# Four graph layers on one core: where nodes' edges are counted, where sums of logits are fetched, and two tensors for a_dst

## The chip, the cores and the metric

The kernel runs on one core of one Trainium2 chip. The metric is the device time of one execution in microseconds. A core has five engines with a queue of instructions each: PE multiplies matrices, DVE and ACT work on vectors, POOL is used here for iotas, memsets and the gathers of indirect DMAs, and SP issues plain DMAs. Engines wait for one another by semaphores; each takes its own instructions strictly in order.

## What is computed

The graph has 6250 nodes and 106250 edges (50000 in both directions and a loop for each node), sorted by destination. A node's features x have 128 numbers. Cut to what matters:

```python
x = layernorm(x + mlp(concat(segment_sum(edge_attr_128, dst), x)))        # layer 0
h = (1 + eps) * x + segment_sum(x[src], dst)                              # layer 1
h = bn(relu(bn(h @ W1 + b1)) @ W2 + b2);  x = layernorm(x + relu(h + x))
h = relu(mean(x[src], dst) @ W1_l + b1 + x @ W1_r)                        # layer 2, two passes
x = layernorm(x + mean(h[src], dst) @ W2_l + b2 + h @ W2_r)
# layer 3: attention; every node has one more edge to itself, whose attribute is the
# mean of the attributes of its incoming edges
alpha = leaky_relu(a_src[row] + a_dst[col] + a_edge)                      # three heads
attn = softmax of alpha over the edges of one col
x = layernorm(x + (segment_sum(attn * xp[row], col) + gat_bias) @ lin_W + lin_b)
```

The kernel needs the following from the graph alone: for each node how many edges end at it (rcnt, its reciprocal), the number of its first edge (start_of) and of its last one (lasti). For layer 3 it needs the running sum of the edges' logits at each node's last edge (st), and a_dst of a node spread over all its edges.

## The kernel before

Nodes are held in 50 blocks of 125, and worked on in 13 chunks of four blocks. The edges lie 128 to a tile: 831 tiles. The program is recorded in the order in which the Python code runs and then placed by a scheduler of the framework, which estimates times and lets instructions of independent parts pass each other; the order on each engine is fixed when the program is built. Line numbers are those of the profile.

Most of the neighbour sums are a dense product. A matrix of edge counts (all 6250 sources by the first ND = 5000 destinations, `matrix`, bfloat16 in device memory) is built once and multiplied in layers 1 and 2; for the remaining 1250 destinations the rows of source nodes are gathered, 128 edges at a time.

- **Prologue (0 to about 95 us).** Indices are loaded and lists of keys made. Edst, the tensor in device memory to which a_dst will be written, is filled with zeros from `acc0` by ACT's queue.
- **Matrix build and layer 0's edge sums (95 to 485).** A loop over 70 batches `q`: each loads a piece of the 128-wide attributes (SP's queue), forms one-hots (`one_hots`, L352, DVE) and sums edges into `acc0` (PE L341, ACT L343, PE L345, DVE L348). From q=6 on, between the two halves of a batch, four steps of `making` run: two one-hots by DVE (olow and okey, L616), four matmuls (`made`, L643) and ACT's copy to `arena` (L645); a filled half of the arena is stored by ACT's queue. `products` (weights' products of layer 3) runs at q = 8 and 12.
- **Layer 0's MLP (485 to 637).** A loop over the 13 chunks: transposes (L308, copied by ACT L309), matmuls (L755, L756, ReLU by ACT L757; L763), layernorm, and `split` (L377 to L380) of the result into three bfloat16 parts in `xp`, a view of `arena`. Ahead of the loop stands POOL's memset of `xp[96:128]` (L740).
- **Layer 1's neighbours (637 to 1031).** `neighbours` multiplies `xp` with the matrix, streamed in pieces by SP's queue (L845), gathers the remaining rows (`row`, L800, POOL) and sums them as in the build. A hook `each(i)`, called once for every piece, drives two generators beside it: every seventh piece one step of `counting`, every third piece one step of `logits`. `counting` finds for 625 nodes a step how many edges lie before each (POOL's iota L542, seven compares by DVE L544 and L546, five matmuls of one column L536, then L430, L431, L539). `logits` loads the 16-wide attributes (`eat`, POOL's queue L691 and L693, with a memset L690 by POOL where a piece is not full) and multiplies and reduces them on DVE (L683, L684).
- **Layer 1's rest (1031 to 1163).** Two batch norms and matmuls, then a loop over the chunks with the layernorm and `split`. `counted` starts ahead of it with 50 gathers of destinations (`nd`, L436, POOL); in the loop each chunk adds three DVE instructions (L563 to L565), and at the end come start_of, rcnt and lasti. `loops` writes the running sums of logits to device memory as `esum`.
- **Layer 2's first pass (1163 to 1690).** `neighbours` again, with `last_sums` as its hook: one of 50 gathers of esum at lasti (`st`, L665, POOL) for a piece, any left over after it.
- **Layer 2's second pass (1690 to 2160).** `neighbours` with `then(k)` for each chunk: the layernorm, a_src and a_dst, POOL's memsets of the constant columns (xw L1048, ad L1049), and four indirect writes of a_dst to `edst` (L1071, POOL). A write to edst waits until the write before has landed.
- **Fill (2160 to 2223).** Edst is loaded in two DMAs and spread along the edges by scans (L1250, L1254); L1106 adds the edges' logits. Rows of layer 3 (L1090) are prefetched on POOL.
- **Layer 3 (2223 to 3562).** Attention over the tiles.

Of the kernel before, what the change touches and what calls it, by code (L numbers as in the profile page):

```python
# [8 lines left out]
F32 = mybir.dt.float32  # L9
# [200 lines left out]
def by_windows(ctx: ExitStack, tc: tile.TileContext, a: dict, out: bass.AP, consts, ix):  # L210
# [20 lines left out]
    mh = const.tile([128, H, F], F32, name="mh")  # L231
    cb = const.tile([128, F], F32, name="cb")
    x3 = dram.tile([NW, XW], F32, name="x3")
    edst = dram.tile([RB * L, 4], F32, name="edst")
    esum = dram.tile([RB * L, H], F32, name="esum")

    PARTS = [list(range(s, min(s + 2, N // SC))) for s in range(0, N // SC, 2)]
# [168 lines left out]
    mps = keep.enter_context(tc.tile_pool(name="mps", bufs=2, space=bass.MemoryType.PSUM))  # L406
    pp1 = keep.enter_context(tc.tile_pool(name="cps", bufs=1, space=bass.MemoryType.PSUM))
    nc.gpsimd.memset(acc0, 0.0)
    nc.scalar.dma_start(edst.rearrange("(p t) f -> p (t f)", t=L), acc0[:RB, 0:L * 4])
    loan = [NB5 * F // 2]  # L410

    def borrow(shape):
# [111 lines left out]
    def counting(pool, psum):  # L524


        row = tail[:RB, AN:AN + M * PB]
        view = arena[:RB, NB5 * 3 * F + 2 * (AN + M * PB):]
        steps = NB5 // M
        for c in range(steps + 1):  # L530
            if c:
                cs = slice((c - 1) * M, c * M)
                below = view[:, (c - 1) % 2 * M * PB:((c - 1) % 2 + 1) * M * PB]
                p = psum.tile([128, 2 * SC], F32, name="hp1")
                for i in range(M):
                    nc.tensor.matmul(p[:PB, i:i + 1], lhsT=below[:, i * PB:(i + 1) * PB], rhs=oneb,  # L536
                                     start=True, stop=True)
                start_row(n0[:PB, cs], p[:PB, 0:M])
                nc.vector.tensor_copy(n0i[:PB, cs], n0[:PB, cs])  # L539
            if c < steps:  # L540
                below = view[:, c % 2 * M * PB:(c % 2 + 1) * M * PB]
                nc.gpsimd.iota(row, pattern=[[1, M * PB]], base=c * M * PB + 1, channel_multiplier=0,  # L542
                               allow_small_or_imprecise_dtypes=True)
                nc.vector.tensor_scalar(below, row, ix["df"][:, 0:1], None, op0=OP.is_gt)  # L544
                for k in range(1, RT):
                    nc.vector.scalar_tensor_tensor(below, row, ix["df"][:, k:k + 1], below, op0=OP.is_gt, op1=OP.add)  # L546
            yield

    def counted(pool):


        thn = pool.tile([128, NB5], F32, name="node_col")
        nc.gpsimd.iota(thn, pattern=[[PB, NB5]], base=1, channel_multiplier=1,
                       allow_small_or_imprecise_dtypes=True)
        nc.vector.memset(upto[:, 0:1], 0.0)
        nd = pool.tile([128, NB5, 128], I32, name="nd")
        edges_from(a["dst"], n0i[:PB], nd[:PB])
        for blocks in CHUNKS:
            work = yield
            cs, nb = slice(blocks[0], blocks[-1] + 1), len(blocks)  # L560
            up = upto[:PB, 1 + cs.start:1 + cs.stop]
            lt = work.tile([128, 4, F], F32, name="rest")
            nc.vector.tensor_tensor(lt[:PB, :nb], nd[:PB, cs], over(thn[:PB, cs], 128), op=OP.is_lt)  # L563
            nc.vector.tensor_reduce(up, lt[:PB, :nb], AX.X, OP.add)
            nc.vector.tensor_add(up, up, n0[:PB, cs])  # L565

        shift = pool.tile([PB, 2, PB], F32, name="shifts")
        nxt = pool.tile([128, 2], F32, name="nexts")
        for i, by in enumerate((1.0, float(1 - PB))):
            nc.vector.tensor_scalar(nxt[:, i:i + 1], part, by, None, op0=OP.add)  # L570
            nc.vector.tensor_scalar(shift[:, i, :], iota[:PB, :PB], nxt[:PB, i:i + 1], None, op0=OP.is_equal)
        p = (yield).tile([128, 4, F], F32, name="node_p")[:, 0, :]
        start = p[:PB, 0:NB5]
        nc.tensor.matmul(start, lhsT=shift[:, 0, :], rhs=upto[:PB, 1:], start=True, stop=False)
        nc.tensor.matmul(start, lhsT=shift[:, 1, :], rhs=upto[:PB, 0:NB5], start=False, stop=True)
        nc.vector.tensor_copy(start_of[:PB], start)
        nc.vector.tensor_tensor(rcnt[:PB], upto[:PB, 1:], start, op=OP.subtract)
        nc.vector.reciprocal(rcnt[:PB], rcnt[:PB])
        nc.vector.tensor_scalar(lasti[:PB], upto[:PB, 1:], -1.0, None, op0=OP.add)
        yield  # L580
# [82 lines left out]
    def last_sums():  # L663
        for b in range(NB5):
            nc.gpsimd.indirect_dma_start(  # L665
                out=st[:PB, b, :], out_offset=None, in_=esum,
                in_offset=bass.IndirectOffsetOnAxis(ap=lasti[:PB, b:b + 1], axis=0))
            yield

    w1 = load_k(wp, "l0w1", a["L0_gnn_W1"], 2, 512)  # L670
    w2 = load_k(wp, "l0w2", a["L0_gnn_W2"], 4, F)
# [2 lines left out]
    def logits(pool, work):  # L674
# [11 lines left out]
        for c in range(0, L, W):  # L686
            x = work.tile([RB, W, 16], F32, name="eat")
            n = min(W, max(0, E - full - c))
            if n < W:
                nc.gpsimd.memset(x, 0.0)  # L690
            nc.gpsimd.dma_start(x[0:RB - 1], ea[0:full, :].rearrange("(p t) k -> p t k", t=L)[:, c:c + W, :])  # L691
            if n:
                nc.gpsimd.dma_start(x[RB - 1:RB, 0:n, :],  # L693
                                    ea[full + c:full + c + n, :].rearrange("(p t) k -> p t k", p=1))
            held.append((c, x))
            if len(held) > 2:
# [6 lines left out]
    ea = a["edge_attr_128"]  # L703
    of = bases(0, NG, DVE)
    make = making(mkp, mps)
    product = products()
    quads, batches, LATE = ND // SC * 13, (NG + 3) // 4, 6
    for q in range(batches):
        g0 = 4 * q
# [19 lines left out]
        next(sums, None)  # L729
        if q in (8, 12):  # L730
            next(product)
    for _ in make:
        pass
    keep.close()

    with tc.tile_pool(name="l0w", bufs=2) as work, \
            tc.tile_pool(name="hps", bufs=4, space=bass.MemoryType.PSUM) as hps, \
            tc.tile_pool(name="yps", bufs=2, space=bass.MemoryType.PSUM) as yps, \
            tc.tile_pool(name="tps", bufs=2, space=bass.MemoryType.PSUM) as tp:
        nc.gpsimd.memset(xp[96:128], 0.0)  # L740
        last = None
        for blocks in CHUNKS:
            b0, nb = blocks[0], len(blocks)
# [28 lines left out]

            def last(b0=b0, nb=nb, cs=cs):
                features(xt[:, cs], xn[:PB, b0:b0 + nb, :], tp)
        last()
    l0.close()

    def neighbours(before, take, then, table, after, each=None, bufs=5):
# [89 lines left out]
    with tc.tile_pool(name="l1", bufs=1) as wp:  # L868
# [37 lines left out]
        with tc.tile_pool(name="l1d", bufs=1) as dp, tc.tile_pool(name="l1e", bufs=4) as two, \  # L906
# [5 lines left out]
                for m in range(2):  # L912
                    stats(s1[:, m], k, hidden(k, m, hps))

            logit, indices = logits(dp, two), counting(dp, hps)

            def each(i):
                if i % 7 == 1:
                    next(indices, None)
                if i % 3 == 2:  # L920
                    next(logit, None)

            neighbours(None, take, then, tables[0], len(matrix), each)
            for x in (logit, indices):
                for _ in x:
                    pass
        counts = ExitStack()
        degrees = counted(counts.enter_context(tc.tile_pool(name="l1c", bufs=1)))
        next(degrees)
        with tc.tile_pool(name="l1p", bufs=1) as lp, tc.tile_pool(name="l1w", bufs=2) as work, \  # L930
                tc.tile_pool(name="hps", bufs=3, space=bass.MemoryType.PSUM) as hps:
            looped = loops(lp, hps)
# [2 lines left out]
            for k in range(len(PARTS)):  # L935
# [10 lines left out]
                stats(s2, k, hp[:, :w])  # L946
                if k in (2, 4):
                    next(looped)
        batchnorm(2, s2, b2, g2, be2)
        with tc.tile_pool(name="l1x", bufs=2) as work, tc.tile_pool(name="zps", bufs=3, space=bass.MemoryType.PSUM) as zps, \  # L950
                tc.tile_pool(name="tps", bufs=2, space=bass.MemoryType.PSUM) as tp:
            last = None
            for blocks in CHUNKS:
# [6 lines left out]
                z = nodes(h0[:, cs], nb, zps)  # L960
                if last is not None:
                    last()
                degrees.send(work)
                layernorm(xn[:PB, b0:b0 + nb, :], z)
                keep_nodes(nc.sync, tables[1], blocks, xn[:, b0:b0 + nb, :])
                split(xn[:PB, b0:b0 + nb, :], blocks, work)
# [1 line left out]
                def last(b0=b0, nb=nb, cs=cs):  # L968
                    features(xt[:, cs], xn[:PB, b0:b0 + nb, :], tp)
            last()  # L970
            degrees.send(zps)
        counts.close()

    with tc.tile_pool(name="l2", bufs=1) as wp, tc.tile_pool(name="l2w", bufs=2) as work, \
# [47 lines left out]
                keep_nodes(nc.scalar, tables[2], blocks, pn[:, b0:b0 + len(blocks), :])  # L1024
            return late

        ends = last_sums()
        neighbours(before, take, None, tables[1], len(matrix), lambda i: next(ends, None))
        for _ in ends:
            pass  # L1030


    with tc.tile_pool(name="l2bw", bufs=2) as work, \
            tc.tile_pool(name="tps", bufs=2, space=bass.MemoryType.PSUM) as tp, \
            tc.tile_pool(name="aps", bufs=1, space=bass.MemoryType.PSUM) as aps:
        for blocks in CHUNKS:
            split(pn[:PB, blocks[0]:blocks[-1] + 1, :], blocks, work)

# [3 lines left out]
        def then(k):  # L1042
            blocks = CHUNKS[k]
            b0, nb = blocks[0], len(blocks)
            x = xn[:PB, b0:b0 + nb, :]
            xw = work.tile([128, 4, XW], F32, name="xw")
            ad = work.tile([128, 4, 4], F32, name="ad")
            nc.gpsimd.memset(xw[:, :, F + H:XW], 1.0)  # L1048
            nc.gpsimd.memset(ad, 0.0)  # L1049
            s = nodes(xt[:, cols(k)], nb, tp)  # L1050
            y = work.tile([128, 4, F], F32, name="y3")
            y = y[:PB, :nb, :]
# [16 lines left out]
            lrelu(lg)  # L1069
            for j in range(nb):  # L1070
                nc.gpsimd.indirect_dma_start(  # L1071
                    out=edst, out_offset=bass.IndirectOffsetOnAxis(ap=start_of[:PB, b0 + j:b0 + j + 1], axis=0),
                    in_=ad[:PB, j, :], in_offset=None)
            keep_nodes(nc.scalar, x3, blocks, xw)

# [21 lines left out]
        fetch(b)  # L1097
    with tc.tile_pool(name="fill", bufs=1) as fp, \
            tc.tile_pool(name="fps", bufs=2, space=bass.MemoryType.PSUM) as pp:
        ed = fp.tile([RB, L, 4], F32, name="ed")  # L1100
        for p0, p1, queue in ((0, 112, nc.sync), (112, RB, nc.scalar)):
            queue.dma_start(ed[p0:p1].rearrange("p t f -> p (t f)"),
                            edst[p0 * L:p1 * L, :].rearrange("(p t) f -> p (t f)", t=L))
        filled = fp.tile([RB, L, H], F32, name="filled")
        along(tc, consts, ix["first"], [ed[:, :, h] for h in range(H)], [filled[:, :, h] for h in range(H)], fp, pp)()
        nc.vector.tensor_add(filled, filled, aeb)  # L1106
# [812 lines left out]
```

## Time and profile before

| what | value |
|---|---|
| median of 5 runs | 3557.95 us (3534.11 to 3571.18) |
| profiled execution | 3564.12 us |
| its span | 3562.3 us |
| mean granted TensorE clock | 0.847 |
| busy: PE, DVE, ACT, POOL | 2697.9, 1736.0, 904.2, 1685.0 us |
| DMA | 461.80 MB, 130 GB/s mean |

The span runs from the first to the last recorded instruction; the profiled execution is one run, and its time lies some us beside its span. Busy times overlap, as the engines work side by side. A row of a group of instructions gives the line, engine, operation, output and inputs, shape and count, then the busy time in us and the mean of one in ns, then how long the engine idled before these instructions and what ended it. A row of waits gives the waiting engine, tile and line, what it waited for, and the us in total, the number of times and the longest. "issue" is idle time in which the engine waited for nothing that the profile shows. The granted clock is given as a share of full speed.

### The profile page before, as it was taken

The page shows a single profiled execution, that of the slowest core. Times are in us where ns is not written, and L with a number is a line of the kernel's source. Part 1 is how long each engine was busy: PE and PEld are TensorE (multiplying, and loading weights), DVE is VectorE, ACT ScalarE, POOL GpSimd, SP SyncE. Part 2 cuts the span into 40 slices and gives each one's busy share as a digit, 9 for nine tenths or more (in the row PEclk, how much of TensorE's full clock was granted, in tenths as well). Part 3 has the DMA queues.
Part 4 walks back from the last instruction along what each step waited for, and adds up shares of the span by engine and source line. Part 5 has one row for each costly group of instructions (what it writes and reads, how often), then busy time and mean ns, then how long its engine had stood idle before and what let it go on. Part 6 is the DMA issues. An engine that isn't in the chain of part 4 may idle for free.

```text
span 3562.3 us, 42918 instructions
## 1 busy us (share of the span) xinstructions
PE 2697.9 (76%) x14960; PEld 1648.5 (46%) x14960; DVE 1736.0 (49%) x4633; ACT 904.2 (25%) x1661; POOL 1685.0 (47%) x1690
## 2 busy tenths in 40 slices
PE   2889989799994589999888894666666666666666
PEld 1444456344442135444334342555555555555555
DVE  4877854584138100001211123666666666656666
ACT  0788854000014000002000010222222222222222
POOL 5000020576433764520666425666666666666563
PEclk9888889899995589999888896888777777777777
DMA  5799931676632355553555552222222222222221
GB/s 168 233 302 294 301 133 45 200 237 210 214 102 61 109 160 188 183 176 108 181 167 172 158 173 76 54 57 58 58 56 61 58 57 57 56 56 60 53 58 35
DMA packets 334828, 461.80 MB, mean 130 GB/s; under 512 B 45310, under 2 KB 219166, under 8 KB 334245
## 3 DMA queue, kind: packets, MB, share of 16 engines
q1 hardware_dynamic: 251420, 278.88, 26.1%
q0 software_dynamic: 54912, 105.86, 11.0%
q10 hardware_dynamic: 28270, 74.24, 5.6%
q8 instruction: 119, 1.95, 0.2%
q14 instruction: 107, 0.88, 0.1%
HBM read 375.30 MB, written 83.36 MB: 129 GB/s over the span
## 4 chain that ended last, share of the span: by engine, by line
PE 39%; issue 11%; DVE 10%; another core or an unknown queue 4%; POOL 3%; ACT 1%; DMA 1%; DVEq 0%; ACTq 0%; POOLq 0%; SPq 0%
PE sums L845 17%; PE o L1198 8%; PE w_p L1176 3%; POOL rows L1090 2%; PE o L1148 2%; DVE w L1186 2%; PE yp L1020 1%; PE both L341 1%; DVE mx L1179 1%; PE both L1183 1%; ACT w L1188 1%; DVE w L1171 1%; PE fp L1132 1%; DVE acc L1206 1%
## 5 line engine op out<-in xcount | busy, mean ns | idle before, releaser
L845 PE MATMUL sums<-piece,arena 125*128 125x500 bf16 x4500 | 1036.3, 386 | 62.0 <-issue 50.5
L1090 POOL DMA_INDIRECT rows<-x,srca x831 | 852.8, 1026 | 481.9 <-issue 213.3
L845 PEld LDWEIGHTS <-arena 125*128 125x128 bf16 x4500 | 438.2, 99 | 613.5 <-issue 153.4
L800 POOL DMA_INDIRECT row<-table,srca x549 | 541.4, 986 | 332.1 <-PE both L341 143.9
L1198 PE MATMUL o<-rows,w 128*120 128x132 f32 x2078 | 406.4, 340 | 160.9 <-ACT w L1188 83.4
L1198 PEld LDWEIGHTS o<-rows,w 128*120 128x120 f32 x2078 | 355.4, 239 | 201.5 <-ACT w L1188 104.3
L645 ACT CAST arena<-made 128x1000 bf16<-128x1000 f32 (+1 forms) x260 | 315.9, 1280 | 61.1 <-PE made L643 57.8
L1188 ACT ACTIVATE w<-w 128x720 f32<-128x720 f32 x208 | 167.0, 803 | 639.0 <-DVE w L1186 498.3
L643 PE MATMUL made<-okey,olow 128*128 128x250 bf16 x1000 | 257.6, 400 | 35.5 <-ACT arena L645 17.4
L1179 DVE TENSOR_REDUCE mx<-w_p 120x1 f32<-120x768 f32 x208 | 198.3, 953 | 172.3 <-PE o L1198 70.3
L1176 PE MATMUL w_p<-ident,w 128*120 128x128 f32 x1248 | 231.3, 328 | 22.4 <-issue 16.6
L1183 PE MATMUL both<-ident,mx 120*128 120x120 f32 x208 | 74.1, 356 | 214.6 <-DVE acc L1206 110.5
L1186 DVE TENSOR_TENSOR w<-w,both 128x720 f32<-128x720 f32 x208 | 187.2, 900 | 89.6 <-PE w_p L1176 56.2
L343 ACT COPY by_node<-both 128x128 f32<-128x128 f32 (+1 forms) x48 | 12.8, 266 | 813.2 <-PE both L341 589.4
L1176 PEld LDWEIGHTS w_p<-ident,w 128*120 128x120 f32 x1248 | 189.9, 170 | 62.8 <-issue 30.8
L352 DVE TENSOR_TENSOR onehot<-iota,relg 128x384 f32<-128x384 f32 x118 | 63.9, 544 | 304.3 <-PE both L341 219.1
L1171 DVE TENSOR_TENSOR w<-oh,z 128x720 f32<-128x720 f32 x208 | 187.3, 900 | 14.7 <-PE o L1198 8.0
L643 PEld LDWEIGHTS <-olow 128*128 128x128 bf16 x1000 | 109.9, 119 | 157.3 <-issue 69.1
L716 POOL MEMSET ea<- 128x128 f32 x1 | 0.2, 206 | 362.8 <-DMA ea<-in_edge_attr_dram 362.8
L616 DVE TENSOR_TENSOR okey<-iok,key 128x1000 bf16<-128x1000 bf16 (+1 forms) x260 | 169.8, 653 | 0.0
L1148 PE MATMUL o<-zeros 128*120 128x380 bf16 x416 | 145.2, 400 | 22.5 <-issue 21.9
L348 DVE TENSOR_TENSOR arena<-arena,both 128x32 f32 x183 | 34.2, 187 | 236.2 <-PE both L345 137.2
(286 smaller groups left out, 3387.7 us busy)
## 6 DMA issues: line engine op xcount, KB each, us to landing
piece<-edges SPq DMA_DIRECT2D x300, 625.0 KB
edges<-arena ACTq DMA_DIRECT2D x100, 625.0 KB
ea<-in_edge_attr_dram SPq DMA_DIRECT2D x69, 768.0 KB
loop<-x SPq DMA_DIRECT2D x208, 68.0 KB
rows<-x,srca POOLq DMA_INDIRECT x831
row<-table,srca POOLq DMA_INDIRECT x549
eat<-in_edge_attr_dram POOLq DMA_DIRECT2D x28, 236.0 KB
table<-xn SPq DMA_DIRECT2D x24, 224.0 KB
```

What stands on the lines that cost most here:

```text
L643: nc.tensor.matmul(p[:, i, 0:NB5 * GD], lhsT=o[:, :, i], rhs=w[:, :, i], start=True, stop=True)
L645: nc.scalar.copy(to, p[:, 0:n, 0:NB5 * GD].rearrange("p i (h d) -> p i h d", d=GD))
L800: nc.gpsimd.indirect_dma_start(out=r[:, j, :], out_offset=None, in_=table, in_offset=bass.IndirectOffsetOnAxis(ap=ix["src"][:, t:t + 1], a ...
L845: nc.tensor.matmul(p, lhsT=xp[:PB, h, i, :], rhs=t[:PB, :, (h - h0) * SC:(h - h0 + 1) * SC], start=(h == 0 and i == 0), stop=(h == NB5 - 1 ...
L1090: nc.gpsimd.indirect_dma_start(out=r[:, j, :], out_offset=None, in_=x3, in_offset=bass.IndirectOffsetOnAxis(ap=ix["src"][:, BT * b + j:BT ...
L1148: nc.tensor.matmul(to, lhsT=zeros[:, 0:H * BW], rhs=zeros[:, 0:to.shape[1]], start=True, stop=True)
L1171: nc.vector.tensor_tensor(w, oh.to_broadcast([128, S, H, BW]), z.rearrange("p j (h w) -> p j h w", w=1).to_broadcast([128, S, H, BW]), op= ...
L1176: nc.tensor.transpose(tp[:, j // 3, j % 3 * 128:(j % 3 + 1) * 128], w[:, j, :, :].rearrange("p h w -> p (h w)"), ident)
L1179: nc.vector.tensor_reduce(mx, tp[:, :, 0:384], AX.XY, OP.max)
L1186: nc.vector.tensor_tensor(wf, wf, mb.rearrange("p (j h) w -> p j (h w)", j=1) .to_broadcast([128, S, H * BW]), op=OP.subtract)
L1188: nc.scalar.activation(wf, wf, AF.Exp)
L1198: nc.tensor.matmul(o[:, 0:F + H + 1], lhsT=wf[:, j, :], rhs=rr, start=(j == 0), stop=(j == S - 1))
```

## The change

Five things change. `counting` moves from layer 1's neighbours to the build loop: one step each at q = 15, 20 and so on to 65, with row and view tiles of its own. `counted` moves from layer 1's rest to layer 0's MLP: its gathers ahead of the loop, its DVE work in the loop's chunks, its tail behind it. `last_sums` moves from layer 2's first pass to the middle of layer 1's rest, ahead of the second batch norm. The attributes `eat` are loaded by ACT's queue, and their memset is DVE's. a_dst is written to two tensors in turn, both filled with zeros at the start and added up in the fill; and the constant columns of xw and ad are set once, in tiles with room for three chunks, by DVE.

```diff
-    edst = dram.tile([RB * L, 4], F32, name="edst")
+    edst = [dram.tile([RB * L, 4], F32, name=f"edst{i}") for i in range(2)]
...
-    nc.scalar.dma_start(edst.rearrange("(p t) f -> p (t f)", t=L), acc0[:RB, 0:L * 4])
+    for x in edst:
+        nc.scalar.dma_start(x.rearrange("(p t) f -> p (t f)", t=L), acc0[:RB, 0:L * 4])
...
     def counting(pool, psum):
-        row = tail[:RB, AN:AN + M * PB]
-        view = arena[:RB, NB5 * 3 * F + 2 * (AN + M * PB):]
+        row = pool.tile([RB, M * PB], F32, name="node_row")
+        view = pool.tile([RB, 2 * M * PB], BF16, name="node_below")
...
-                p = psum.tile([128, 2 * SC], F32, name="hp1")
+                p = psum.tile([128, 256], F32, name="counts")
...
     def last_sums():
         for b in range(NB5):
             nc.gpsimd.indirect_dma_start(out=st[:PB, b, :], ..., in_=esum, ...)
-            yield
...
             if n < W:
-                nc.gpsimd.memset(x, 0.0)
-            nc.gpsimd.dma_start(x[0:RB - 1], ...)
+                nc.vector.memset(x, 0.0)
+            nc.scalar.dma_start(x[0:RB - 1], ...)
             if n:
-                nc.gpsimd.dma_start(x[RB - 1:RB, 0:n, :], ...)
+                nc.scalar.dma_start(x[RB - 1:RB, 0:n, :], ...)
...
-    product = products()
+    product, indices = products(), counting(gw, pp1)
     for q in range(batches):
...
+        if q >= 13 and q % 5 == 0:
+            next(indices, None)
-    for _ in make:
-        pass
+    for x in (make, indices):
+        for _ in x:
+            pass
     keep.close()
...
         nc.gpsimd.memset(xp[96:128], 0.0)
+        degrees = counted(cp)
+        next(degrees)
         for blocks in CHUNKS:
...
+            degrees.send(work)
         last()
+        degrees.send(yps)
     l0.close()
...
-            logit, indices = logits(dp, two), counting(dp, hps)
+            logit = logits(dp, two)
             def each(i):
-                if i % 7 == 1:
-                    next(indices, None)
...
-        degrees = counted(counts.enter_context(tc.tile_pool(name="l1c", bufs=1)))
-        next(degrees)
...
                 if k in (2, 4):
                     next(looped)
+            last_sums()
         batchnorm(2, s2, b2, g2, be2)
...
                     last()
-                degrees.send(work)
                 layernorm(xn[:PB, b0:b0 + nb, :], z)
...
-        ends = last_sums()
-        neighbours(before, take, None, tables[1], len(matrix), lambda i: next(ends, None))
-        for _ in ends:
-            pass
+        neighbours(before, take, None, tables[1], len(matrix))
...
+        ads = xws.tile([128, 3, 4, 4], F32, name="ad")
+        xws = xws.tile([128, 3, 4, XW], F32, name="xw")
+        nc.vector.memset(xws[:, :, :, F + H:XW], 1.0)
+        nc.vector.memset(ads, 0.0)
...
-            xw = work.tile([128, 4, XW], F32, name="xw")
-            ad = work.tile([128, 4, 4], F32, name="ad")
-            nc.gpsimd.memset(xw[:, :, F + H:XW], 1.0)
-            nc.gpsimd.memset(ad, 0.0)
+            xw, ad = xws[:, k % 3], ads[:, k % 3]
...
-                    out=edst, out_offset=...
+                    out=edst[j % 2], out_offset=...
...
-        ed = fp.tile([RB, L, 4], F32, name="ed")
-        for p0, p1, queue in ((0, 112, nc.sync), (112, RB, nc.scalar)):
-            queue.dma_start(ed[p0:p1], edst[p0 * L:p1 * L, :])
+        ed, more = (fp.tile([RB, L, 4], F32, name=n) for n in ("ed", "edm"))
+        for to, x, queue in ((ed, edst[0], nc.sync), (more, edst[1], nc.scalar)):
+            for p0, p1 in ((0, 112), (112, RB)):
+                queue.dma_start(to[p0:p1], x[p0 * L:p1 * L, :])
+        nc.vector.tensor_add(ed, ed, more)
```

The order that the scheduler makes of it, on POOL: the nd gathers stand around the memset of `xp[96:128]`, 17 before it and 33 behind it. The 50 st gathers stand between the rows of layer 1 and those of layer 2, which then come in one run. In the build, DVE's compares of `counting` alternate one by one with the one-hots of `making`.

## Prediction

> **What bounds the kernel now.** I read the windows by stage first (us from the span's start; busy time of each engine, granted clock, DMA share and rate; the matrix build, layer 0's MLP, the end of layer 1, then layer 2's two passes):
>
> ```profile
> 300.00:400.00 100.00, 90.11 (x677) 45.14 (x676) 80.36 (x222) 82.82 (x86) 0.00 (x0) 0.86 0.92 301
> 485.00:560.00 75.00, 70.12 (x334) 45.93 (x333) 37.02 (x101) 30.74 (x52) 19.43 (x5) 0.95 0.19 60
> 1085.00:1163.00 78.00, 31.60 (x104) 21.03 (x104) 76.96 (x257) 32.77 (x65) 21.76 (x17) 0.51 0.21 54
> 1200.00:1300.00 100.00, 66.36 (x225) 23.96 (x225) 4.09 (x13) 3.21 (x7) 75.88 (x68) 0.65 0.37 100
> 1300.00:1500.00 200.00, 196.49 (x1070) 96.78 (x1068) 17.80 (x55) 12.41 (x28) 100.74 (x104) 0.99 0.61 194
> 1760.00:2045.00 285.00, 241.71 (x1272) 110.84 (x1270) 44.55 (x190) 15.21 (x37) 160.47 (x170) 0.87 0.54 166
> ```
>
> PE sets the pace nearly everywhere. Three stages are worse than PE needs: the end of layer 1 (1085 to 1163) is DVE's, at 77 of 78 us; 1200 to 1300 has PE at 66% and a clock of 0.65, where the same loop 100 us later runs at 98% and 0.99; and 1760 to 2045 is alike in mild form. In both, POOL is the busy one. The build is PE's, with DVE and ACT close behind.
>
> Next the groups by line (busy, mean ns | idle before) of the moved work:
>
> ```profile
> L546 DVE SCALAR_TENSOR_TENSOR arena<-arena,df 119x625 bf16<-119x625 f32 x45 | 39.0, 866 | 0.4
> L563 DVE TENSOR_TENSOR rest<-nd,node_col 125x512 f32<-125x512 int32 (+1 forms) x13 | 8.6, 665 | 0.1
> L564 DVE TENSOR_REDUCE upto<-rest 125x4 f32<-125x512 f32 (+1 forms) x13 | 8.6, 661 | 0.0
> L436 POOL DMA_INDIRECT nd<-in_dst_dram,n0i x50 | 63.3, 1265 | 15.1 <-issue 14.5 <-DVE xn L956 0.3 <-DVE rstd L298 0.3
> L665 POOL DMA_INDIRECT st<-esum,lasti x50 | 59.9, 1199 | 66.7 <-DVE lasti L579 51.7 <-issue 15.0
> L1071 POOL DMA_INDIRECT edst<-ad,start_of x50 | 59.8, 1196 | 157.3 <-DMA edst<-ad,start_of 76.2 <-issue 46.3 <-DVE xw L1067 19.2
> ```
>
> A gather costs POOL 1.2 us and 0.3 us of issue, 1.5 in all: the 50 nd gathers are 75 us, the 50 st gathers again. Then the chains of waits, of the build (first two lines), of 1163 to 1300 (third), of 1690 to 2160 (the rest):
>
> ```profile
> DVE olow L616 <- PE made L643: 44.5, 100, 1.1
> PE made L643 <- DVE olow L616: 13.1, 23, 0.9
> ...
> PE sums L845 <- issue: 29.7, 31, 2.2
> ...
> POOL edst L1071 <- DMA edst<-ad,start_of: 76.2, 32, 4.4
> DVE xw L1066 <- POOL xw L1048: 53.6, 10, 9.5
> PE both L341 <- issue: 29.5, 38, 2.4
> PE ad_p L1061 <- ACT x3t L309: 13.8, 2, 7.0
> ```
>
> Last, the timeline of POOL where layer 0's MLP begins (start, us):
>
> ```profile
> 488.62 16.09 POOL L740 MEMSET arena<- 32x19200 bf16 x1 [43.55 <-ACT xc L309]
> 504.78 1.38 POOL L792 MEMSET arena<- 128x1532 f32 x1
> 506.11 0.67 POOL L542 IOTA arena<- 119x625 f32 x1
> ```
>
> **The sum, against the profiled execution:** 3564.1 us, a span of 3562.3 and 1.8 around it. That is 6.2 above the median of 3557.95, so the total below is lowered by 6. A measurement of this kernel can tell about 0.5%, 18 us.
>
> **Start.** Zeroing edst is doubled, 1.7 MB more by ACT's queue beside the first loads; at the 253 GB/s of 100 to 200 that is 7 us at most. I take +2 (0 to 6).
>
> **Build.** Ten counting steps come in, one every fifth batch from q=15. One is 0.55 us (L544), six L546 of 0.87 and some 0.55 us of small ones: 6.3 us of DVE, 63 in all. DVE idles 82 us between 100 and 485 (by windows of 100, 100, 100 and 85 us), but a batch takes 6.0 us, of which DVE is free 1.3. So one step fills the free time of five batches and DVE stands at 97%. It hides only if DVE works ahead: it does, its 44.5 us of idle before L616 is waiting for PE to give a buffer back, and three make buffers at 1.46 us each let it lead by 4.4 us of the 6.3. But the changed program alternates L546 with the one-hots, PE's 13.1 us of waiting for them grows, and the sums' chain through L348 lies behind the same queue. Bounds: 0, if all hides, and +63, if none does. I take +20, nearer to the low end, because DVE's lead covers two thirds of a step; for the range 5 to 45.
>
> **Layer 0's MLP.** Thirteen us of counting leave DVE, 13 x 1.5 us of degrees come in; DVE is busy 37 of 75, so both cost nothing (up to 19 if not covered). What costs is POOL's order: the 16.1 us memset of arena, which the first split (ACT L377) needs, now stands behind 17 nd gathers. 484 + 17 x 1.5 = 509.5, and 16.1 more: 525.6. Before, the split ran at 508.69, and only because DVE had waited 8.56 us for the iota behind the memset; now it could run at 502.5 and waits to 525.6. Behind it on ACT are the evictions of the next chunk's features and hidden units, so PE, after some 8 us of work that needs none, stands about 15 us, where it stood 4.9: +12 (0 to 20). The other 33 gathers take 50 us beside 110 us of PE work: hidden.
>
> **Layer 1's neighbours.** DVE loses 48 us of counting, the eat loads leave POOL for ACT, which is idle there. PE is busy 364 of 394 us, and of its 30 only the DVE waits (6.8 at 702) and part of the crawl at 660 to 673 can go: −8 (−20 to +6; the loss if ACT, waiting for an eat buffer, holds by_node's copy, L343). [...]
>
> **Layer 1's rest.** From the DVE-bound 78 us go L563 to L565, 8.6 + 8.6 + 1.9, and a tail of some 2 us: −20. Late next is PE at 32 and ACT at 33, so nothing takes it back (−26 to −8). The st gathers come here: esum's write is issued at 1062.9, so they run from 1065 to 1140, and the rows are due at about 1150. If POOL's 1265 ns of nd beside this DVE work (986 ns for a row) holds for them, they end at 1144, still in time. [...]
>
> **Layer 2's first pass.** Five st gathers go from before the first row: −7. The slow stretch 1196 to 1241 and 1260 to 1287 coincides with POOL issuing 45 st and the rows without pause; PE then starts one instruction per 0.7 us. Of 137 us from 1163 PE idles 51. The start of layer 1's pass, rows alone, idles 19 of 63 at a clock of 0.85 and 10 of the next 120. So about 25 of the 51 go, and of PE's 86 us at 0.66 about 15 more: −40 with the −7 counted in (−60 to −5). The low end is the case in which rows alone crowd PE as much.
>
> **Layer 2's second pass.** POOL waits 76 us for the write before to land, and while it does it can't issue rows or the memset of xw, for which DVE waits 53.6, and PE through ACT 13.8. Two tensors halve the first (each waits for the one before last), three standing tiles end the second. PE idles 67 of 470 us; 13.8 + half of the 29.5 of L341 + a little clock: −30 (−60 to 0).
>
> **Fill.** Edst's last write moves ahead of the rows of layer 3 that stood between: before 2184.7, now some 6 us earlier. Two loads of 1.7 MB instead of one (9.2 us at 185 GB/s; two at the 301 of the build 11.3): +2; one add of 119x3584, from L1106's 3.0 us for 119x2688: +4. Sum 0 (−6 to +8). Layer 3 is as it was.
>
> 2 + 20 + 12 − 8 − 20 − 40 − 30 + 0 = −64; 3564 − 64 − 6 = 3494.
>
> **Rivals.**
> A. As forecast, 3494 (3440 to 3538): 0.62.
> B. PE's crawl comes of POOL's row bursts themselves, and the gathers were hidden: for it, layer 1's pass crawls at 660 to 673 with no st gather. Layer 2 gives the −7 and −13.8 alone: 2 + 20 + 12 − 8 − 20 − 21 = −15, so 3543 (3535 to 3560): 0.18.
> C. Slower: DVE becomes the build's bound. Its place is 170 to 480, its price up to 6.3 us a step, +63, and the path's L348 behind it. With the start's 2 and layer 0's 12 that is 77 against 28 from layer 1; it decides from where layer 2 gives under 49 us. With 30 there: +19, 3577 (3555 to 3590): 0.20. For it: DVE at 81% with 16% more to do. Against it: the 44.5 us in which DVE waits for PE.
>
> The range for 8 in 10 takes all of A but its lowest end, B, and C to 3570: 3445 to 3570; A's own range stands above. Faster by over 0.5% (under 3540): nearly all of A, a third of B and none of C: 0.66. Within: the rest of A, half of B, a tenth of C: 0.13. Slower: 0.21.
>
> **What would show it.** Right: the build ends 15 to 30 us later with PE's wait for DVE olow grown from 13.1; POOL's 16 us memset starts near 510 and PE has a gap of 15 us behind it; no st gather among layer 2's rows, and PE over 80% in the 137 us from its start; the edst wait under 40. Wrong: a build longer by 45 or more, rows still crawling after the first 25, or a first row later than 10 us after layer 1's end.

## The result: a little slower, and the profile after

The changed kernel takes 3582.91 us in the median of 35 runs, the kernel before 3565.04 in 61: a ratio of 1.0052, 95% interval 1.004 to 1.0065. The forecast was 3494, with a range of 3445 to 3570. The profiled execution has a span of 3585.2 us against 3562.3. The kernel before took 3242 to 3248 us beside e1 to e4, e9 to e12, e17 and e18 (group S, where PE's products have next to no idle time put down to issue: in e4 at most 0.8 us before `sums` and 0.1 before layer 3's `o`) and 3551 to 3565 beside the others and in the traces here (group L, where the kernel before has 50.5 and 77.1), so stages are compared only within a group, and kernels by their ratio to the kernel before.

The stages of the two profiled executions, marked off by PE's instructions (first and last product of the build, last of layer 0, first and last of each pass over the matrix), in us:

| stage | before | after | measured | forecast |
|---|---|---|---|---|
| start to the first make | 96.9 | 102.9 | +6.0 | +2 |
| build | 382.3 | 407.3 | +25.0 | +20 |
| layer 0's MLP | 151.8 | 161.8 | +10.0 | +12 |
| from there to layer 1's pass | 10.5 | 21.3 | +10.8 | none |
| layer 1's pass (neighbours) | 389.8 | 454.3 | **+64.5** | **−8** |
| layer 1's rest and layer 2's first pass | 625.6 | 542.9 | −82.7 | −60 |
| to the second pass | 33.2 | 34.7 | +1.5 | 0 |
| layer 2's second pass | 470.4 | 456.5 | −13.9 | −30 |
| fill, to layer 3's first z | 53.0 | 56.8 | +3.8 | 0 |
| layer 3 | 1348.8 | 1346.7 | −2.1 | 0 |

One stage has turned the gain into a loss: without its +64.5 the stages add up to −42. The windows of the changed kernel (columns as in the prediction; the build, then the middle of layer 1's pass), and last the middle of that pass in the kernel before:

```profile
300.00:400.00 100.00, 83.51 (x649) 44.25 (x648) 87.16 (x233) 77.71 (x78) 1.97 (x3) 0.74 0.83 276
820.00:920.00 100.00, 64.47 (x299) 28.14 (x296) 53.60 (x80) 0.80 (x3) 34.99 (x36) 0.82 0.56 174
...
820.00:920.00 100.00, 98.75 (x566) 46.19 (x564) 29.97 (x72) 1.33 (x5) 62.52 (x62) 1.00 0.67 213
```

In 820 to 920 of the changed kernel no engine is busy for more than 65 of 100 us; there is a wait, not a load. Over the whole pass PE idles 77 us where it idled 26. The waits from 680 to 1105 name the cause:

```profile
DVE product L683 <- DMA eat<-in_edge_attr_dram: 86.0, 21, 8.6
...
PE both L341 <- DVE arena L348: 32.5, 3, 11.7
...
PE both L345 <- ACT by_node L343: 11.8, 2, 9.4
```

DVE stands 21 times, in all 86 us, before an attribute load; behind it in DVE's queue is the addition of a row's sum (L348), and PE waits for that. The other side is ACT's issues of these loads (L691 loads 118 partitions, L693 the last one; count, then the time that an issue holds ACT, min/median/max in ns), and ACT's timeline:

```profile
L691 ACTq DMA_DIRECT2D eat<-in_edge_attr_dram x28: 239/258/7906, 681.9 to 894.7; - x28
L693 ACTq DMA_DIRECT2D eat<-in_edge_attr_dram x17: 393/4547/9402, 682.2 to 816.4; - x17
```

```profile
705.15 5.96 ACTq L693 DMA_DIRECT2D eat<-in_edge_attr_dram  x1
...
736.04 7.33 ACTq L693 DMA_DIRECT2D eat<-in_edge_attr_dram  x1
743.72 0.27 ACT L343 COPY by_node<-both 128x128 f32<-128x128 f32 x1 [62.70 <-DMA row<-table,srca]
```

Issuing a load took POOL 0.53 to 0.57 us. On ACT most issues of the 118 partitions take 0.26 us (the longest 7.9), but the issue of the one partition that follows holds ACT for 4.5 us in the median; the 45 issues together hold it for 120 us. The copy of by_node, which PE needs, stands behind them: at 743.72 it follows a 7.33 us issue at once. What the queue itself does is in the DMA part of 697 to 700 (packets, MB, share of the 16 engines), with the queue of POOL's loads in the kernel before, 671 to 675, in the last line:

```profile
q0 software_dynamic: 64, 0.13, 13.2%
q10 hardware_dynamic: 67, 0.13, 11.6%
...
q0 software_dynamic: 370, 0.81, 68.3%
```

ACT's queue (q10) moved nothing but these loads and had 11.6% of 16 engines: not quite two. From POOL (q0) the same loads had 68.3%. Theory W, in the next section, puts this down to the count of partitions. The kernel before has a load of 112 partitions in its fill, the one of edst by SP's queue: from 2188 to 2192 that queue (q1), with nothing else to move, had 89.7%. The experiments test it.

### The profile page after: what moved, and what is told of

It reads as the page before. It is cut to its first block, busy times and chain, and to the rows that moved or that the text cites. A ratio compares the mean times of both kernels' runs of the same rounds, so it can differ in the third digit from the quotient of the medians.

```text
span 3585.2 us, 42898 instructions
## 1 busy us (share of the span) xinstructions
PE 2684.4 (75%) x14960; PEld 1648.5 (46%) x14960; DVE 1753.6 (49%) x4648; ACT 909.8 (25%) x1661; POOL 1650.1 (46%) x1607
## 4 chain that ended last, share of the span: by engine, by line
PE 56%; DVE 15%; issue 10%; DMA 7%; another core or an unknown queue 6%; ACT 4%; ACTq 1%; DVEq 1%; POOL 0%; SPq 0%; POOLq 0%
PE sums L852 22%; PE o L1197 9%; DMA eat<-in_edge_attr_dram 4%; PE w_p L1175 4%; PE made L644 3%; ACT arena L646 2%; PE o L1147 2%; PE sums L341 2%; DVE mx L1178 1%; PE both L341 1%; PE yp L1019 1%; DVE w L1185 1%; DVE node_below L547 1%; PE hp L760 1%
## 5 line engine op out<-in xcount | busy, mean ns | idle before, releaser
L807 POOL DMA_INDIRECT row<-table,srca x549 | 532.2, 969 | 558.1 <-PE both L341 282.5
L1170 DVE TENSOR_TENSOR w<-oh,z 128x720 f32<-128x720 f32 x208 | 187.4, 901 | 10.5 <-PE o L1197 7.3
L348 DVE TENSOR_TENSOR arena<-arena,both 128x32 f32 x183 | 34.2, 187 | 281.8 <-PE both L345 137.0
```

What stands on the lines that cost most here:

```text
L807: nc.gpsimd.indirect_dma_start(out=r[:, j, :], out_offset=None, in_=table, in_offset=bass.IndirectOffsetOnAxis(ap=ix["src"][:, t:t + 1], a ...
L1170: nc.vector.tensor_tensor(w, oh.to_broadcast([128, S, H, BW]), z.rearrange("p j (h w) -> p j h w", w=1).to_broadcast([128, S, H, BW]), op= ...
```

## The experiments

**What the loads cost.** In e1, on the changed kernel:

```diff
-            nc.scalar.dma_start(x[0:RB - 1], ea[...][:, c:c + W, :])
+            for p0, p1 in ((0, 112), (112, RB - 1)):
+                nc.scalar.dma_start(x[p0:p1], ea[...][p0:p1, c:c + W, :])
```

> The changed kernel with one edit: the attribute loads stay on ACT's queue, but each is issued as 112 partitions and 6 partitions instead of 118 at once. In the changed kernel the first pass of layer 1 (first to last L852 product) took 454 us against 390 before, and an eat load of 118 packets ran with two packets of 84 ns at a time. Theory W (few DMA engines): a count of 118 splits over two engines only, 112 over sixteen; loads land in 2 to 3 us instead of about 8, and ACT's issues stop taking 4.5 us each. Then the pass returns to 385 +- 10 and the whole kernel to about 3515 (-65). Theory Q (order on ACT's queue): ACT is held by waiting for eat buffers whatever the load's width; then the pass stays above 435 and the kernel above 3560. Theory B (the lost time is the matrix build's): the pass matters little, kernel above 3570.

Ratio 0.9763 (0.9727 to 0.98), from 1.0052: the shape of one load decides the sign. The pass takes 351 us in group S. In group L, e8, which has the same loads, takes 373, against 453 in the changed kernel (e6) and 392 in the kernel before (e5): a fall of 80 us, where some 70 were expected. ACT's issues, a window of the pass and the DMA part of 672 to 676 in e1:

```profile
L692 ACTq DMA_DIRECT2D eat<-in_edge_attr_dram x56: 271/326/508, 671.3 to 798.3; - x56
L694 ACTq DMA_DIRECT2D eat<-in_edge_attr_dram x17: 229/262/275, 672.0 to 749.4; - x17
```

```profile
780.00:880.00 100.00, 100.00 (x564) 46.28 (x563) 45.05 (x87) 1.33 (x5) 61.08 (x62) 1.00 0.78 238
```

```profile
q10 hardware_dynamic: 283, 0.49, 45.2%
```

The same queue now uses 45% of the engines, an issue takes 0.33 us in the median, all 73 together 23 us, and PE is busy without a gap. Theory W holds in the loads' shape (how many engines carried a load of 112 no page of e1 shows), theory Q falls: ACT's order is unchanged and costs nothing when the loads land.

> The changed kernel with the attribute loads and their memsets back on POOL's queue, all else as changed. Theories W and Q alike: the pass of layer 1 returns to 380 to 395 us (390 before), and the kernel to about 3510 (-70): the forecast's other parts alone (start +6, build +25, layer 0 +21, layer 1's rest and layer 2's first pass -83, second pass -14). Theory B: no change, above 3570.

E2, the loads back on POOL: 0.9827 (0.9804 to 0.985), the pass 375 us. The kernel's gain is as expected; ACT's queue with 112 partitions is 24 us better in the pass than POOL's (both in group S). So moving the loads was right, and their shape was the fault.

> The kernel before with one part of the change: the attribute loads on ACT's queue in loads of 118 partitions, their memset on DVE. Theories W and Q: the pass of layer 1 grows from 390 to 440 to 470 us and the kernel by 40 to 80, to about 3620; counting on DVE runs in this pass too, so it may be more than in the changed kernel. Theory B: within 10 us of before.

E3, the kernel before with this one part: 1.0224 (1.0204 to 1.0245), the pass 448 us. The part alone makes the loss.

**Layer 0's memset.** E4 adds one edit to e1: `nc.vector.memset(xp[96:128], 0.0)`.

> As the kernel with loads of 112 and 6 partitions, and the memset of xp[96:128] ahead of layer 0's MLP given to DVE, which idles there, instead of POOL, where it stands behind 17 gathers. If PE's gap of 15.5 us in layer 0 comes of that order, layer 0's MLP falls from 162 us to about 150 (-10 to -14), and the kernel is 10 us faster than its neighbour without this edit. If the gap has another cause (DVE's layernorm, the gathers of nd), it stays within 3 us.

Layer 0's MLP falls from 162.0 to 145.7 us, ratio 0.9713 (0.9681 to 0.9744). In the changed kernel POOL's memset ran at 536.43, behind the 17 gathers, and PE stood 15.53 us before a transpose of xn, as forecast:

```profile
536.43 16.11 POOL L743 MEMSET arena<- 32x19200 bf16 x1
...
552.68 0.47 PE L308 MATMUL feat_p<-ident,xn 125*128 125x125 f32 x1 [15.53 <-DVE xn L300]
```

DVE does the memset in 8.06 us where POOL took 16.09, and the stage is 6 us shorter than in the kernel before (151.5 in e3).

**The build.** E5 profiles the kernel before, e6 the changed one, e7 moves the counting steps (`if 1 <= q <= 11`) and e8, below, ends the degrees earlier, both on top of e4.

> The kernel before, unchanged, profiled on the chip of the next three runs, so that stages are compared on one chip. No theory tells of it; on the chip of the first four runs the unchanged layer 3 took 1182 us where it took 1402 in the first trace, so its stages there stand to the first trace's as the chip does: layer 1's pass, which PE and DMA bound alike, near 390.

> The changed kernel, unchanged, beside the same chip's kernel before. Theory W: layer 1's pass 60 to 70 us longer than before, layer 1's rest and layer 2's first pass together 70 to 85 shorter, the build 20 to 25 longer, layer 0 with the way to the next pass 20 longer, the second pass 14 shorter: 0 to 1% slower in all.

> As the kernel with loads of 112 and 6 partitions and the memset on DVE, and the ten counting steps put into batches 1 to 11 instead of 15 to 65. Until the first make, PE waits for the attributes to load, and DVE idles half of the time. If the build's 25 us come of DVE's 63 us of counting beside the one-hots, then from the first to the last make it returns to 383 +- 4, the first make comes 0 to 10 us later as DVE's lists of keys wait behind some compares, and the kernel gains 10 to 25 us on the neighbour without this edit (0.9713 of before on another chip). If the build is longer for another reason (the own tiles, the clock), the step from first to last make stays above 395.

E6 is at 1.0056 (1.0026 to 1.0086), its stages up to layer 3 as in the table within 2 us. E7, at 0.988 (0.9815 to 0.9945), went against its expectation: first to last make took 427 us, not 383. The scheduler put most compares not ahead of the first make but right behind it, and DVE became the bound for 60 us; then the pace is that of before (from 260 to 310 PE is busy 45.71 of 50). A window of e7:

```profile
110.00:160.00 50.00, 25.93 (x188) 14.18 (x188) 48.40 (x112) 19.42 (x18) 3.94 (x6) 1.00 0.24 77
```

So it is DVE's compares that cost, and the denser, the more. E9 does the opposite on e4: a `yield` after every compare, and one compare (two in every fourth batch) a batch from q=6.

> As the kernel with loads of 112 and 6 partitions and the memset on DVE, and the counting steps cut into single compares: about one L548 of 0.87 us a batch, through batches 6 to 69, instead of six in every fifth. DVE has 1.3 us free in a batch of 6.0. If the build's +24 comes of DVE's clumps (6.3 us against a lead of 4.4), first to last make falls from 407 to 383 to 392. If it comes of the mere sum of DVE's work (97% busy), it stays at 400 to 408. The kernel: 10 to 20 us faster than its neighbour in the first case.

First to last make takes 385 us, against 407 in e4 and 385 in e3, whose build is the one of before (all group S). DVE is busy 94 of 100 and PE 90.5, and the ratio is the lowest of all: 0.9647 (0.9629 to 0.9665). Its window answers to 300 to 400 above:

```profile
300.00:400.00 100.00, 90.51 (x710) 48.20 (x709) 94.26 (x254) 86.55 (x87) 1.98 (x3) 0.83 0.93 308
```

It is the clumps, not the sum: 63 us of DVE work disappear in a stage in which DVE had 82 free.

**The way to layer 1's pass.** E8 finishes the degrees by chunk 10.

> As the kernel with loads of 112 and 6 partitions and the memset on DVE, and the degrees finished by chunk 10 of layer 0's MLP instead of behind its last chunk (two chunks' degrees in chunks 7, 8 and 9). If the first pass of layer 1 starts 10 us later than before because its rows and pieces wait for the memory of the gathered destinations (POOL's row waits for start_of), then the time from layer 0's last product to the pass falls from 20 us to 10 to 12, and the kernel gains 8 to 10. If something else holds it, it stays at 18 to 21.

Ratio 0.9788 (0.9736 to 0.984), and the gap stayed: 22.6 us, with start_of ready 22 us before the first row gather. So the degrees' end isn't what holds it in e8. In e8 and in the changed kernel alike PE's order has a row's sums (L341) ahead of the first piece, and PE waits 8 to 10 us for the first rows; in the kernel before it began with the piece. That order isn't the whole cause: in the changed kernel PE then waits 1.50 us more for the piece. The first piece itself is issued later: 11 us after layer 0's last product in the changed kernel and 10 in e8, 6 in the kernel before. What holds it stays open; no run tries it.

**Layer 2's second pass.** On e4, e10 writes a_dst to one tensor again, e12 has POOL's memsets of xw and ad again.

> As the kernel with loads of 112 and 6 partitions and the memset on DVE, with a_dst in one tensor again (one zero fill, two loads, no addition). If the two tensors are what shortened layer 2's second pass (472 to 455), the pass goes back to 465 to 480; the first make comes 5 to 6 us earlier without the second zero fill, the fill is 4 to 10 us shorter. If POOL's waits for edst cost PE nothing, the pass stays within 4 us and the kernel gains 5 to 15.

> As the kernel with loads of 112 and 6 partitions and the memset on DVE, with POOL's memsets of xw and ad for every chunk again. The forecast gave their removal 14 us (PE's waits for x3t) of the second pass's gain. If it holds, the pass grows from 455 to 465 to 472; if the gain is the two tensors' alone, it stays within 4 us.

E4's pass took 399.6 us, e10's 417.3, e12's 412.1; the ratios are 0.9745 (0.9726 to 0.9765) and 0.9759 (0.9736 to 0.9783), whose intervals overlap with e4's, so the stage has to decide. It does: the seven group S kernels with both parts, e4 among them, take 394 to 402. Both parts are needed. Either one alone gains little: with both as before, e3's pass takes 416.9, so the standing tiles without the two tensors (e10) gain nothing, and the two tensors without the standing tiles (e12) gain some 5 of the 17. The waits in the pass show why, in the changed kernel, in e10 and in e12:

```profile
POOL edst L1068 <- DMA edst<-ad,start_of: 24.6, 14, 3.1
...
POOL edst L1068 <- DMA edst<-ad,start_of: 79.4, 32, 4.3
...
DVE xw L1063 <- POOL xw L1045: 107.5, 10, 23.7
```

E10's first make comes at 92.2 us against 96.7, its fill is 53.6 us against 56.1: the second tensor's price is 7 us.

E16, on e9, zeroes the tensors in 112 and 7 partitions.

> As the kernel with single compares spread over the build, and the zero fill of both tensors issued as 112 and 7 partitions instead of 119. If 119 partitions go by few DMA engines and hold up the first attributes, the first make comes 2 to 5 us earlier (96.7 or 102.9 with the fill at once, 92.2 with one tensor); if the bytes alone count, it stays. The kernel: 0 to 6 us.

First make at 94.1 us, against 102.9 in e14 and 100.3 in e13, which have the same start but for this, and 96.9 in the kernel before, which zeroes half as much. So it wasn't the bytes. The DMA parts of 40 to 50, of e14 and then of e16, agree:

```profile
q10 hardware_dynamic: 127, 1.72, 42.2%
...
q10 hardware_dynamic: 203, 2.37, 65.0%
```

With 119 partitions the fill has 42.2% of the engines, and from 50 to 60 it still runs and SP's loads of the attributes have 11.3%; with 112 it is over by then, and SP's loads have 86.8%. The kernel's ratio, 0.9689 (0.9649 to 0.9729), can't tell it from e14's (0.9726).

**Layer 1's rest and layer 2's first pass.** E11, on e4, and e14, on e9, put `last_sums` back in the pass's hook.

> As the kernel with loads of 112 and 6 partitions and the memset on DVE, with the 50 gathers of esum back in layer 2's first pass. The forecast gave their move 40 us of the 83 that layer 1's rest and layer 2's first pass lost together, and the degrees' move 20. If that holds, the two together grow by 35 to 60 us over the kernel with the gathers moved (543); if POOL's gathers were hidden beside the pass (rival B), by less than 10, and the 83 are due to DVE's degrees alone.

> As the kernel with single compares spread over the build, with the 50 gathers of esum back in layer 2's first pass. Theory M: within 5 us of its neighbour without this edit where PE shows no issue gaps; where it shows them (some 60 us before the products over the whole trace, as in the first trace), 5 to 30 us lost by the forecast's crowding.

Ratios 0.97 (0.9681 to 0.9719) and 0.9726 (0.9673 to 0.9779); layer 1's rest with layer 2's first pass moved by 2 us (e11 against e4) and 4 (e14 against e16). But neither tells anything of the gathers: the scheduler left all 50 in layer 1's rest (in e14 from 1070 to 1155), as lasti is known early now. E13, on e9, instead holds a tile of 25.6 KB a partition through the rest, where the nd gathers lay before; e15 is the kernel before again, in group L.

> As the kernel with single compares spread over the build, and a tile of 25.6 KB a partition held open through layer 1's rest, where the kernel before had the gathered destinations; four numbers of a row are written at its start and one at its end, no other work. In the kernel before, the first piece of layer 2's first pass was issued behind the last chunk's split (L380), at 1166 where that split ends; in the changed kernel it waits only for products of the pass before, and the products start 62 us after layer 1's pass, while DVE still does the rest. Theory M (memory): the first product of the pass comes 120 to 145 us after layer 1's pass instead of 62, and layer 1's rest with layer 2's first pass grows by 50 to 70 us, the kernel as much. Theory D (DVE's degrees): both stay within 8 us.

> The kernel before, unchanged, for stages on the chip of these runs. Its layer 1's rest with layer 2's first pass: 625 where PE shows issue gaps, 575 to 590 where not.

E15: 628 us for the two stages together; e14, with the memory free, 545 (549 in e16); e13 564, at 0.9759 (0.9708 to 0.981). The first product comes 139 us after layer 1's pass (62 in e14), as theory M has it, but the loss is 15 to 19 us and not 50 to 70. SP's timeline in e13: its loads of pieces begin behind the last chunk, as before, where in e14 products of the pass already run beside the chunks.

```profile
1134.82 7.98 SPq L271 DMA_DIRECT2D table<-xn  x6
...
1146.31 23.58 SPq L852 DMA_DIRECT2D piece<-edges  x6
```

E17 and e18, on e9, bind the gathers to the last chunk (their offsets pass through `scalar_tensor_tensor(lastj, xn[last block], 0.0, lasti, mult, add)`), e18 with the memory held too.

> As the kernel with single compares spread over the build, and the 50 gathers of esum bound to the last chunk of layer 1's rest (their offsets go through one more DVE instruction that reads the chunk), so that they stand among layer 2's rows as in the kernel before: 6, 5, 5, 6, 25 and 3 between the rows. Forecast's theory (POOL's unbroken gathers crowd PE): layer 1's rest with layer 2's first pass grows from 546 by 25 to 50 us, with issue gaps before the products, where PE shows such gaps at all (the kernel before near 3555); where it does not (near 3245), by less than 12. Rival B (the gathers were hidden): less than 8 in either.

> As the run before it, with the tile held in layer 1's rest as well, so that POOL's order is the one of before (5 gathers, 24 rows, 27 gathers, 12 rows, 18 gathers). The stages then stand as before but for the degrees' work on DVE: layer 1's rest with layer 2's first pass 605 to 620 by the forecast's theory where PE shows issue gaps (564 with the memory held alone), 560 to 575 by rival B.

The two stages take 514.5 us in e9, 555.1 in e17, 573.7 in e18 and 585.8 in e3, where they are as before; the ratios are 0.9758 (0.9737 to 0.9778) and 0.9845 (0.9827 to 0.9863). So the gathers' place is worth 41 and the memory 19, and 12 are left for the degrees' work, which no run isolates. All this is group S, without issue gaps, where the expectation had less than 12 for the gathers, and rival B less than 8: both missed. What the gathers cost there is POOL's time, for which the rows wait (e9, then e17, 1060 to 1300):

```profile
PE both L341 <- DMA row<-table,srca: 16.1, 6, 7.2
...
PE both L342 <- DMA row<-table,srca: 50.3, 17, 17.8
```

In group L the same parts are worth 83 us (e5 against e6). Of these only the memory's was measured there; the gathers' was not. And the crawl that the forecast put down to the gathers is still there without them. In the changed kernel POOL issues only rows from 1302 to 1335, and PE is busy for 15 of the 33 us, at a clock of 0.62; in the 137 us from the pass's start it is busy for 95, or 69%, where the kernel before had 86:

```profile
1210.00:1347.00 137.00, 94.88 (x451) 46.42 (x452) 66.43 (x214) 33.53 (x68) 103.00 (x88) 0.83 0.46 125
1302.00:1335.00 33.00, 15.20 (x54) 8.14 (x54) 3.76 (x13) 2.01 (x5) 21.18 (x23) 0.62 0.21 63
```

## Why the prediction was wrong, point by point

- **Layer 1's neighbours, −8 (−20 to +6), was the step that failed**; it came out at +64.5. The term took ACT's idleness for a free queue and priced only the loads' place in ACT's order; the time of the loads themselves stood at nothing. In its place the runs showed the loads' shape: 118 partitions by ACT's queue had 11.6% of the engines, DVE waited 86 us for them, and their issues held ACT for 120 us. The range's bad end did name ACT holding by_node's copy, but for want of an eat buffer, and at +6. The kernel before had one transfer that could have warned, the zero fill of edst: 119 partitions by ACT's queue, 35.8% of the engines from 40 to 50. With 112 partitions the term is −18 to −20 (e8 against e15 and e5), at the good end of the range. With 112 partitions the move gained 24 us in the pass (e1 against e2), where the term had 8 for it and the counting together; no run shows whether they are POOL's 25 us of issuing (28 loads of 0.56 and 17 of 0.54 us in the kernel before), or loads that land sooner.
- **The build, +20**, measured +25, is right in size, and e9 shows that DVE's clumps make it. The sign named for it failed: PE's wait for olow fell from 13.1 us to 2.0. PE's waits for DVE as a whole grew, from 19 to 34 us, at the one-hots of the sums, at L348 and at the counting's own compares:

```profile
PE sums L341 <- DVE onehot L352: 9.6, 12, 1.2
PE counts L537 <- DVE node_below L547: 7.5, 9, 1.3
PE made L644 <- DVE xt L348: 6.6, 15, 0.8
```

- **Rival C** has the measured 3583 in its range (3555 to 3590), by luck: it put the loss into a build 63 us longer, and the build grew by 25.
- **Layer 0, +12**, measured +10, the memset behind 17 gathers, as worked out. The way to the pass, +10.8, was in no term, and its cause stays open.
- **Layer 1's rest and layer 2's first pass, −20 and −40**, measured −82.7. That the gathers came out at 41 in e17 is luck in part: the mechanism was to be PE's crawl, but in group S the cost was rows waiting for POOL, and in group L the crawl stayed (69% where the sign asked for over 80). Rival B was right that PE crawls with no gather of esum about, and wrong that the gathers were hidden. What is left for the degrees is 12 and not 20. Unforeseen were 15 to 19 us for the memory that the nd tile had held, which kept the pass from starting beside the chunks; some 10 us of group L's 83 stay unexplained. Of the 50 gathers of esum, which ran beside DVE's work, 37 took the 1.2 us that they took among the rows, and 13 took 1.3 to 2.8: 10 us in all (70.1 against 59.9). What held the 13 no run isolates.
- **Layer 2's second pass, −30**, measured −14 in the first traces, and −26 to −32 in e8 against e15 and e5: the size is right to within what the profiles of before differ (470 to 484). The sign held (the wait for edst fell from 76.2 to 24.6 us). The sum added the two steps' gains as if each stood by itself, and e10 and e12 show that it takes both. (PE's idle time in this pass is 64 us by the windows, not 67.)
- **Start and fill** were mis-sized by 4 each: +6 because of 119 partitions, +4 because the two loads of edst took 19.5 us (2198.2 to the addition at 2217.7), not 11.3; some of that came back, as the last write to edst, counted from the end of the second pass, stood 9 us earlier and not 6.

With −18 in place of +64.5 the measured stages would add up to −60, against −64 forecast. That closeness is luck in part: layer 1's rest with layer 2's first pass gained 23 more than forecast, and the second pass, the way to layer 1's pass, the build, the start and the fill together lost more than that. E8, with loads of 112 and also the memset on DVE, gives 3482.

## What to carry to other kernels

When a load moves to another engine's queue, look at its partition count as well as at the queue: here a cut at 112, with the rest in a load of its own, turned a loss into a gain (1.0052 to 0.9763). Work given to a busy engine hid here when it came in pieces smaller than the 4.4 us that the prediction had worked out as the engine's lead, one compare of 0.87 us a batch (a build of 385 us); in clumps of 6.3 us it didn't (407). A tile's memory is an order too: a tile held where the next stage's buffers go made that stage begin 77 us later here (139 against 62), and cost 15 to 19.

## What the runs showed of the hardware

- A plain load of 118 partitions by ACT's queue ran with 11.6% of the 16 DMA engines (697 to 700), one of 112, with its rest of 6, with 45.2% (e1, 672 to 676), and a store of 119 with 42.2% (e14, 40 to 50). From POOL's queue the loads of 118 had 68.3% (before, 671 to 675).
- Behind a load of 118 partitions the issue of the one partition held ACT for 4.5 us in the median and 9.4 at most (the changed kernel); behind loads of 112 and 6 it took 0.26 (e1).
- DVE set 32 x 19200 bfloat16 to zero in 8.06 us (e4), POOL in 16.09 (before).
- A gather of 125 rows of esum took POOL 1.2 us among layer 2's rows (before). Beside DVE's work at the end of layer 1, 13 of 50 took longer, up to 2.78 us, and 37 did not (the changed kernel).
